# A gated feed-forward layer made as [feature, token] behind a saturated TensorE, with half of its butterflies on GpSimd

## The chip, the cores and the metric

The kernel runs on one core of a Trainium2 chip. The metric is the device time of one execution in microseconds, as the median of several runs. TensorE is written PE, VectorE DVE, ScalarE ACT, GpSimd POOL and SyncE SP; PEld is TensorE's loading of stationary weights.

## The reference

Four batches of 512 tokens with 512 features pass through two layers; each has an attention part and a feed-forward part, gated by a tanh and added to `x`. The change lies in the feed-forward of the first layer, and in the weights of the second one's. The first feed-forward is

```python
def fwht(x):            # normalized Walsh-Hadamard transform along the last axis (length a power of 2)
    ...
def act_quant(x):       # per token
    scale = 127.0 / clip(max(abs(x), axis=-1, keepdims=True), 1e-5)
    return clip(round(x * scale), -128.0, 127.0) / scale
def weight_quant(w):    # ternary
    scale = clip(mean(abs(w)), 1e-5)
    return clip(round(w / scale), -1.0, 1.0) * scale
def h_bitlinear(x, w):
    return einsum('bsh,oh->bso', act_quant(fwht(x)), weight_quant(w))
gate = h_bitlinear(h, w_gate)          # 512 -> 2048
up = h_bitlinear(h, w_up)              # 512 -> 2048
out = h_bitlinear(silu(gate) * up, w_down)   # transform over 2048, then 2048 -> 512
x = x + tanh(g_ffn[0]) * out
```

with `h` the layer norm of `x`. The second feed-forward has the same ternary weights and 8-bit activations, no Hadamard transform, and one weight matrix `w_gv` for both halves.

## The kernel before

Tokens are worked on in tiles of 128; a batch has four. Three strands of work exist.

- `attention` is the second layer's attention: 4 batches of 8 pairs of heads with 4 steps each, 128 steps. It is written as a generator and sets the beat of the program. Its PE work is f32 (`pqh` L769, `pb` L784, `pr` L755, `pss` L828, `ppt` L850, `pc` L858, `po` L870). In a pair, DVE finds the row maxima `nm` (L836), ACT exponentiates (L839) and scales (L842), DVE multiplies `ro` and `rs` by the tables (L792, L794, L797) and POOL adds them (L798); PE's `pr` needs these sums.
- The background. For batches 1 to 3 `before(b)` makes first `adjacency(b)` (the first layer's attention, mostly `max` and `match_replace` on DVE at L454 and L459) and then `feed0(b)`, the first feed-forward. Then `last_weights` quantizes the second feed-forward's weights (called w1) and makes `feed1` of batches 0 to 2. Each of these generators yields estimated costs, and a loop over the attention's steps (L994) takes so many of their pieces as are due. `hidden_T(b)`, which starts a batch's attention, needs the batch's `feed0`.
- The start and the end. Batch 0's adjacency and `feed0`, and the quantization of the first feed-forward's weights, stand ahead of the attention; `feed1` of batch 3 stands behind it. There the flag `alone[0]` is true, more PSUM banks and buffers are lent to the feed-forwards, and `quick` is true in `feed0`.

The program order gives priorities; a scheduler with a cost model then puts the instructions of each engine in an order at build time. On the chip every engine takes its own instructions in that order, and an instruction that waits holds up what stands behind it.

`feed0(b)` first makes, for each tile, `zq`: the normalized, transformed, quantized and transposed activations as [feature, token] in bf16, and the columns `dg` and `du` (one scale for each token). Then `tiles` weaves `gated` of tile j with `back` of tile j - 1 (`woven`, one piece of each in turn).

`gated` makes the inner layer as [token, feature]: in each of four blocks of 512 features, `pg` and `pu` are four accumulated products each, with `zq` stationary and the ternary fp8 weights `wa` moving, 512 columns wide. ACT makes `sg` = silu(dg * pg) out of PSUM, the scale being one number a partition (L312); DVE multiplies by `pu` into `ya` (L313).

`back` then transforms over 2048 features. Its upper four levels are butterflies between chunks of 128 features, an addition and a subtraction of 128x1024 each, on DVE (L556). Its lower seven levels are a product with a 128x128 Hadamard matrix, for which `ya` must be [feature, token]: PE transposes 16 chunks into `ph` (L562), ACT copies them to `yT` (L564), PE multiplies into `pzh` (L568), ACT scales into `yb` (L569). `projected` quantizes, turns by DMA (L202) and multiplies by `wd` (L404).

The background has two PSUM banks while `alone[0]` is false (`bg_ps`, tag `bg`): `pg`, `pu`, `ph`, `pzh` and `pd` of the feed-forwards and the adjacency's products share them. `front_t` gives three and `gate_t` two buffers of 128x512.

`ternary` quantizes weights: a sum of absolute values by ACT (L239), then for each 128x2048 piece a scaling with a rounding constant (L252) and a sign (L253) on ACT. `hold` is true for the first feed-forward's weights, whose pieces stay in SBUF, and false for w1, whose twelve pieces are loaded twice.

Of the kernel before, what the change touches and what calls it, by code (L numbers as in the profile page):

```python
# [34 lines left out]
def flamingo_kernel(  # L35
# [37 lines left out]
    def bg_ps(name):  # L73
        return psb.tile([P, 512], F32, tag="bg", name=name)
# [22 lines left out]
    def back_t(name):  # L97
        return two_k("back", 2, name)
# [121 lines left out]
    def ternary(specs, names, hold):  # L220


        found = []

        def piece(src, inner, i, name):
            t = big(f"{name}{i}")
            marks["load"] = nc.sync.dma_start(
                t if inner == 1 else t.rearrange("p (c o) -> p c o", c=inner), src(i)
            )
            return t  # L230

        for (src, inner, n, dst, count), name in zip(specs, names):
            acc = small.tile([P, n], F32, tag=f"wacc{n}", name=f"acc_{name}")
            held = []
            for i in range(n):
                t = piece(src, inner, i, f"sa_{name}")
                held.append(t)
                junk = bp.tile([P, FF], BF, tag="q", name=f"ja_{name}{i}") if hold else t
                nc.scalar.activation(junk, t, AF.Abs, accum_out=acc[:, i : i + 1])  # L239
                yield 4.0  # L240
            tot = small.tile([P, 1], F32, tag="wtot", name=f"tot_{name}")
            nc.vector.tensor_reduce(tot, acc, AX.X, ALU.add)
            pt = bg_ps(f"pt_{name}")
# [4 lines left out]
            nc.vector.reciprocal(inv, sc)  # L248
            found.append(sc)
            for i in range(n):  # L250
                t = held[i] if hold else piece(src, inner, i, f"sb_{name}")
                nc.scalar.activation(t, t, AF.Identity, scale=inv, bias=magic[:, 0:1])  # L252
# [47 lines left out]
    def gated(u, zq, wa, dg, y):  # L300

        for o in range(4):
# [10 lines left out]
            nc.vector.tensor_tensor(y[:, o * 512 : (o + 1) * 512], sg, pu, ALU.mult)  # L313
            yield 0.9

    reached = []

    def tiles(name, ready, wa, back, spread):
# [4 lines left out]
        def gate(j):  # L323
            zq, dg, du = ready[j]
            y = big(f"ya_{name}_{j}")
            return gated(f"{name}_{j}", zq, wa, dg, y), back(j, y, du)

        def go(gen, parts):
            for _ in range(parts):
# [175 lines left out]
    def feed0(b, w):  # L505
# [44 lines left out]
        def back(j, ya, du):  # L550
            u = f"f{b}_{j}"
            yb = big(f"yb_{u}")

            for src, dst, g in ((ya, yb, 8), (yb, ya, 4), (ya, yb, 2), (yb, ya, 1)):
                for args in butterfly(src, dst, "p (g t q) -> p g t q", {"g": g}):
                    nc.vector.tensor_tensor(*args)  # L556
                    yield 1.3
            for k in range(4):
                pt = bg_tr(f"ph_{u}_{k}")
                for c in range(4):  # L560
                    at = (4 * k + c) * P
                    nc.tensor.transpose(pt[:, c, :], ya[:, at : at + P], ident)  # L562
                hT_ = back_t(f"yT_{u}_{k}")
                nc.scalar.copy(hT_, pt.rearrange("p c q -> p (c q)"))  # L564
# [579 lines left out]
```

## Time and profile before

| | us |
|---|---|
| median of 3 runs | 2050.27 (2046.98 to 2051.11) |
| the profiled execution | 2050.43 |
| its span in the trace | 2048.7 |
| PE busy | 1834.1 (90%) |
| DVE busy | 1584.0 (77%) |
| ACT busy | 1128.1 (55%) |
| POOL busy | 337.0 (16%) |

Mean granted PE clock: 0.973. Busy times are of one core's engines within the span. An f32 product shows as two records, one for each pass. A matmul's duration contains its way through the array, so the spacing of starts, not the duration, tells how fast PE takes them. In a row of a group, the numbers after the count are the busy time, the mean duration in ns and the idle time before these instructions with what ended it. A wait is put down to what came last.

The stages of the span: batch 0 and the first weights until about 260 us; adjacency of batch 1 to 457, its feed0 to 660; of batch 2 to 874 and 1073; of batch 3 to 1288 and 1488; w1's quantization to 1600; feed1 of batches 0 to 2 beside the attention to about 1960; then the last batch's feed1.

### The profile page before, as it was taken

What the parts mean: (1) busy time and instruction counts of PE and PEld (TensorE: products, weight loads), DVE (VectorE), ACT (ScalarE), POOL (GpSimd) and SP (SyncE); (2) the same over time, 40 slices, a digit from 0 to 9 for tenths busy, and PEclk for the clock granted to TensorE, in tenths of its full rate; (3) what the DMA queues carried; (4) which work ended last, traced back from release to release, by engine and by line L of the source; (5) the groups of instructions that cost most, each with busy time, mean ns of one, the idle gap of its engine ahead of it and who ended that gap; (6) DMA issues with size and microseconds to landing.
All of it is one profiled execution on the core that took longest, in us unless ns stands there. A gap on an engine that the chain in (4) does not pass through costs nothing. (4 is left out here: it accounts for less than half of the span.)

```text
span 2048.7 us, 20950 instructions
## 1 busy us (share of the span) xinstructions
PE 1834.1 (90%) x6890; PEld 854.8 (42%) x6890; DVE 1584.0 (77%) x3233; ACT 1128.1 (55%) x1883; POOL 337.0 (16%) x316
## 2 busy tenths in 40 slices
PE   1268799989999999999999999999989999999898
PEld 0035534434444444444444444445443444444333
DVE  7989599987775999976678999766745756866775
ACT  6935454455644455454454554545699565555544
POOL 3020031123101122130121221301211210101000
PEclk9779899999999999999999999999999999999999
DMA  7451021111112222111122121111666112222111
GB/s 274 150 179 38 1 77 42 56 50 32 44 35 48 86 73 73 38 39 35 43 53 84 57 84 47 34 35 38 212 224 235 55 38 71 68 54 66 21 31 42
DMA packets 115548, 151.77 MB, mean 74 GB/s; under 512 B 57456, under 2 KB 68080, under 8 KB 112368
## 3 DMA queue, kind: packets, MB, share of 16 engines
q1 hardware_dynamic: 109968, 134.51, 22.3%
q0 software_dynamic: 4320, 14.16, 1.9%
q10 hardware_dynamic: 1152, 1.77, 0.2%
q8 instruction: 55, 0.90, 0.2%
q14 instruction: 53, 0.43, 0.1%
HBM read 117.90 MB, written 19.92 MB: 67 GB/s over the span
## 5 line engine op out<-in xcount | busy, mean ns | idle before, releaser
L798 POOL TENSOR_TENSOR ro<-ro,rs 128x512 f32<-128x512 f32 x192 | 256.5, 1339 | 1151.8 <-DVE rs L794 704.3
L839 ACT ACTIVATE pp<-pss,nm 128x512 f32<-128x512 f32 x256 | 174.5, 685 | 242.9 <-DVE nm L836 242.2
L769 PE MATMUL pqh<-hT,wq 128*128 128x512 f32 x512 | 238.6, 602 | 5.1 <-ACT pp L839 5.0
L858 PE MATMUL pc<-pT,kv 128*128 128x512 f32 x512 | 231.8, 597 | 1.2 <-ACT pT L851 1.2
L870 PE MATMUL po<-om,cxo 128*128 128x512 f32 x512 | 230.7, 596 | 0.0
L836 DVE TENSOR_REDUCE nm<-pss 128x1 f32<-128x512 f32 x256 | 167.5, 681 | 50.5 <-PE pss L831 50.1
L784 PE MATMUL pb<-qh,wc 128*128 128x512 f32 x384 | 190.9, 614 | 13.1 <-ACT qh L774 8.2
L454 DVE MAX8 m<-work 128x8 f32<-128x512 f32 x304 | 198.2, 681 | 0.6
L459 DVE MATCH_REPLACE8 work<-m,work 128x512 f32<-128x512 f32 x288 | 193.0, 675 | 0.1
L842 ACT ACTIVATE pp<-pp,rsm 128x512 f32<-128x512 f32 x256 | 178.1, 722 | 22.1 <-DVE rsm L841 22.0
L851 ACT COPY pT<-ppt 128x512 f32<-128x512 f32 x256 | 142.3, 590 | 37.3 <-PE ppt L850 37.3
L850 PEld LDWEIGHTS ppt<-ident,pp 128*128 128x128 f32 x1024 | 118.8, 142 | 92.4 <-issue 37.3
L850 PE MATMUL ppt<-ident,pp 128*128 128x128 f32 x1024 | 148.1, 279 | 6.0 <-ACT pp L842 2.8
L875 DVE SCALAR_TENSOR_TENSOR x<-po,gt,x 128x512 f32<-128x512 f32 x128 | 94.4, 743 | 75.5 <-PE po L870 74.8
L828 PE MATMUL pss<-kr,qr 64*128 64x512 f32 x256 | 144.3, 645 | 4.6 <-ACT pp L839 3.9
L831 PE MATMUL pss<-kr,qr 64*128 64x512 f32 x256 | 144.4, 645 | 1.0 <-DVE ro L792 0.5
L769 PEld LDWEIGHTS pqh<-hT,wq 128*128 128x128 f32 x512 | 93.0, 191 | 124.1 <-issue 86.8
L870 PEld LDWEIGHTS po<-om,cxo 128*128 128x128 f32 x512 | 94.4, 190 | 115.1 <-issue 97.0
L858 PEld LDWEIGHTS pc<-pT,kv 128*128 128x128 f32 x512 | 93.7, 190 | 111.5 <-issue 97.2
L792 DVE TENSOR_TENSOR ro<-pb,cos_q 128x512 f32<-128x512 f32 x192 | 130.5, 680 | 10.8 <-PE pb L784 9.9
L863 ACT COPY cxo<-pc 128x512 f32<-128x512 f32 x64 | 37.6, 588 | 149.6 <-PE pc L858 149.6
L755 PE MATMUL pr<-ro,wr 128*64 128x512 f32 x192 | 99.2, 612 | 15.3 <-POOL ro L798 12.5
(266 smaller groups left out, 3012.6 us busy)
## 6 DMA issues: line engine op xcount, KB each, us to landing
wq<-in_wqh SPq DMA_DIRECT2D x64, 256.0 KB, 2.6
om<-omd SPq DMA_DIRECT2D x64, 256.0 KB, 2.8
wc<-in_wkcq SPq DMA_DIRECT2D x32, 384.0 KB, 3.1
krd<-krs POOLq DMA_DIRECT2D x32, 256.0 KB, 2.4
kr<-krd SPq DMA_DIRECT2D x32, 256.0 KB, 2.7
sa_w1v<-in_gvT SPq DMA_DIRECT2D x8, 1024.0 KB, 5.8
sb_w1v<-in_gvT SPq DMA_DIRECT2D x8, 1024.0 KB, 5.1
wr<-in_wqr SPq DMA_DIRECT2D x32, 192.0 KB, 2.4
```

What stands on the lines that cost most here:

```text
L454: nc.vector.max(m8[j], cur[j])
L459: nc.vector.match_replace(works[j], m8[j], cur[j], GONE)
L769: nc.tensor.matmul(pq, self.wqs[i][:, c, :], hT[self.b][:, c, :], start=(c == 0), stop=(c == NC - 1),)
L784: nc.tensor.matmul(pb, self.wc[:, at : at + P], self.qhs[i if i < 2 else o], start=True, stop=True)
L798: nc.gpsimd.tensor_tensor(ro, ro, rs, ALU.add)
L831: nc.tensor.matmul(*args, start=True, stop=True)
L836: nc.vector.tensor_reduce(nm, pss[i], AX.X, ALU.max, negate=True)
L839: nc.scalar.activation(pp, pss[i], AF.Exp, bias=nm, accum_out=sm)
L842: nc.scalar.activation(pp, pp, AF.Copy, scale=rs)
L850: nc.tensor.transpose(pt[:, l, :], pp[:, l * P : (l + 1) * P], ident)
L858: nc.tensor.matmul(pc, kv[self.b][:, l, :], self.pT[i][:, l, :], start=(l == 0), stop=(l == NT - 1),)
L870: nc.tensor.matmul(po, self.cxo[i][:, j * P : (j + 1) * P], self.oms[i], start=(i == 0), stop=(i == 1),)
```

## The change

Three edits.

1. `gated_turned` takes the place of `gated` in `feed0` of batches 1 to 3. It makes the inner layer as [feature, token]: the weights are stationary, `zq` moves, 128 columns at a time, so a block has 32 products instead of 8. The gate's scale now differs from column to column. A row of it is made once a tile: `dg` spread over 128 columns on DVE, turned by one f32 product with the identity, copied by ACT. DVE multiplies `pg` by this row, ACT applies silu in SBUF, DVE multiplies by `pu`. `back` then needs no transposes and no copies for these batches: `ya` goes to the Hadamard product as it is.
2. The subtraction of each butterfly goes to POOL for all tiles of batches 1 to 3 and for tiles 1 and 2 of batch 0. The additions stay on DVE.
3. The scaling of w1's pieces (L252, where `hold` is false) goes from ACT to DVE.

```diff
@@ ternary
-                nc.scalar.activation(t, t, AF.Identity, scale=inv, bias=magic[:, 0:1])
+                if hold:
+                    nc.scalar.activation(t, t, AF.Identity, scale=inv, bias=magic[:, 0:1])
+                else:
+                    nc.vector.tensor_scalar(t, t, inv, MAGIC, ALU.mult, ALU.add)
@@ new function
+    def gated_turned(u, zq, wa, dg, y):
+        row = front_t(f"dgr_{u}")
+        nc.vector.tensor_scalar(row[:, :P], ones, dg, None, ALU.mult)
+        pt = bg_ps(f"pdg_{u}")
+        nc.tensor.matmul(pt[:, :P], row[:, :P], ident, start=True, stop=True)
+        nc.scalar.copy(row[:, P : 2 * P], pt[:, :P])
+        row = row[:, P : 2 * P].unsqueeze(1).to_broadcast([P, 4, P])
+        for o in range(4):
+            pg = gate_ps(f"pg_{u}_{o}")
+            pu = gate_ps(f"pu_{u}_{o}")
+            for pw, at in ((pg, FF + o * 512), (pu, o * 512)):
+                for f in range(4):
+                    cols = slice(at + f * P, at + (f + 1) * P)
+                    for c in range(NC):
+                        nc.tensor.matmul(
+                            pw[:, f * P : (f + 1) * P], wa[:, c, cols], zq[:, c, :],
+                            start=(c == 0), stop=(c == NC - 1),
+                        )
+            sg = gate_t(f"sg_{u}_{o}")
+            nc.vector.tensor_tensor(
+                sg.rearrange("p (f t) -> p f t", f=4), pg.rearrange("p (f t) -> p f t", f=4), row, ALU.mult
+            )
+            nc.scalar.activation(sg, sg, AF.Silu)
+            nc.vector.tensor_tensor(y[:, o * 512 : (o + 1) * 512], sg, pu, ALU.mult)
+            yield 0.9
@@ tiles
-            return gated(f"{name}_{j}", zq, wa, dg, y), back(j, y, du)
+            made = gated_turned if spread and not alone[0] else gated
+            return made(f"{name}_{j}", zq, wa, dg, y), back(j, y, du)
@@ feed0, back
+            shared = not quick or j in (1, 2)
...
-                for args in butterfly(src, dst, "p (g t q) -> p g t q", {"g": g}):
-                    nc.vector.tensor_tensor(*args)
+                for k, args in enumerate(butterfly(src, dst, "p (g t q) -> p g t q", {"g": g})):
+                    (nc.gpsimd if k and shared else nc.vector).tensor_tensor(*args)
                     yield 1.3
             for k in range(4):
-                pt = bg_tr(f"ph_{u}_{k}")
...
-                hT_ = back_t(f"yT_{u}_{k}")
-                nc.scalar.copy(hT_, pt.rearrange("p c q -> p (c q)"))
+                if quick:
...
+                else:
+                    hT_ = ya[:, 4 * k * P : 4 * (k + 1) * P]
```

More of the change, by code (lines that the diff above doesn't have):

```diff
@@ L552, in back @@
             yb = big(f"yb_{u}")
+            shared = not quick or j in (1, 2)
             for src, dst, g in ((ya, yb, 8), (yb, ya, 4), (ya, yb, 2), (yb, ya, 1)):
-                for args in butterfly(src, dst, "p (g t q) -> p g t q", {"g": g}):
-                    nc.vector.tensor_tensor(*args)
+                for k, args in enumerate(butterfly(src, dst, "p (g t q) -> p g t q", {"g": g})):
+                    (nc.gpsimd if k and shared else nc.vector).tensor_tensor(*args)
                     yield 1.3
             for k in range(4):
-                pt = bg_tr(f"ph_{u}_{k}")
-                for c in range(4):
-                    at = (4 * k + c) * P
-                    nc.tensor.transpose(pt[:, c, :], ya[:, at : at + P], ident)
-                hT_ = back_t(f"yT_{u}_{k}")
-                nc.scalar.copy(hT_, pt.rearrange("p c q -> p (c q)"))
+                if quick:
+                    pt = bg_tr(f"ph_{u}_{k}")
+                    for c in range(4):
+                        at = (4 * k + c) * P
+                        nc.tensor.transpose(pt[:, c, :], ya[:, at : at + P], ident)
+                    hT_ = back_t(f"yT_{u}_{k}")
+                    nc.scalar.copy(hT_, pt.rearrange("p c q -> p (c q)"))
+                else:
+                    hT_ = ya[:, 4 * k * P : 4 * (k + 1) * P]
                 pz = bg_ps(f"pzh_{u}_{k}")
```

## The prediction

> **What bounds the kernel now.** First the page's slices, to see which engine is full where.
>
> ```profile
> PE   1268799989999999999999999999989999999898
> ...
> DVE  7989599987775999976678999766745756866775
> ACT  6935454455644455454454554545699565555544
> POOL 3020031123101122130121221301211210101000
> ```
>
> A digit is 51 us. From slice 6 to 36 TensorE (PE) is full whatever the other engines do. VectorE (DVE) fills three times (an adjacency each, batches 1 to 3) and is at 6 to 7 between them, where feed0 runs; ScalarE (ACT) reaches 9 once, around 1500 us. Next, the busy time by stage: the columns are PE, weight load, DVE, ACT, POOL, then granted clock.
>
> ```profile
> 457.00:660.00 203.00, 194.83 (x811) 95.88 (x811) 140.42 (x234) 98.73 (x178) 33.61 (x32) 0.97 0.16 40
> ...
> 874.00:1073.00 199.00, 193.53 (x821) 96.64 (x822) 141.97 (x237) 98.61 (x182) 37.84 (x32) 1.00 0.17 44
> ...
> 1288.00:1488.00 200.00, 192.84 (x819) 96.31 (x819) 142.43 (x239) 111.81 (x196) 36.92 (x31) 1.00 0.30 86
> 1488.00:1600.00 112.00, 104.46 (x331) 46.30 (x330) 60.73 (x134) 109.65 (x146) 21.62 (x17) 0.97 0.62 211
> ```
>
> The first three are feed0 of batches 1 to 3: PE 96%, DVE 70%, POOL 18%. The last is w1's quantization, ACT 98% busy. Busy PE is not PE at full pace, so I priced each PE record of a stage at the closest spacing the timeline shows for its kind (0.429 us for a 512-column f32 pass, 0.215 for 512 fp8 columns, 0.109 for a 128-column f32 pass) and divided by the stage: 0.87, 0.91 and 0.89 in the feed0 stages, 0.83 in w1's, 0.915 from 1600 to 1900. So PE's own work sets about nine tenths of the time, and in w1's stage ACT takes a further share. The chain of waits reaches back only to 1695 us and says nothing of the stages changed. Last, the groups that the change touches (count, then busy and mean ns):
>
> ```profile
> L556 DVE TENSOR_TENSOR yb_f<-ya_f 128x1024 f32<-128x1024 f32 x64 | 77.0, 1233 | 3.7 <-PE ph_f L562 3.6
> ...
> L313 DVE TENSOR_TENSOR ya_f<-sg_f,pu_f 128x512 f32<-128x512 f32 x64 | 43.6, 682 | 25.5 <-PE pu_f L307 21.3 <-ACT sg_f L312 4.2
> ...
> L562 PE MATMUL ph_f<-ident,ya_f 128*128 128x128 f32 x256 | 40.7, 289 | 0.4 <-DVE ya_f L556 0.3
> ...
> L564 ACT COPY yT_f<-ph_f 128x512 f32<-128x512 f32 x64 | 37.0, 584 | 26.1 <-PE ph_f L562 26.1
> ...
> L252 ACT ACTIVATE sb_w1v<-sb_w1v,magic,wi_w1v 128x2048 f32<-128x2048 f32 x8 | 16.7, 2098 | 0.3 <-DVE wi_w1v L248 0.3
> ```
>
> **Part 1, the layer turned (12 tiles).** Removed: 12 x 16 transposes on PE at 0.109 = 20.9 us, and 48 ACT copies x 0.584 = 28 us. ACT is half busy here, so the copies count nothing. Split: each of 48 blocks had 8 products of 512 columns (8 x 0.215 = 1.72 us) and gets 32 of 128 columns, each with new weights. The nearest row is the bf16 transpose, also 128 columns with a weight load each:
>
> ```profile
> 2006.79 0.83 PE L207 MATMUL ptq_hg<-identb,q_g 128*128 128x128 bf16 x12
> 2007.46 0.38 PE L307 MATMUL pg_g<-wa_w,zq_g 128*128 128x512 fp8e4 x1
> ```
>
> Twelve go in 0.67 us: 0.056 each, though a load alone lasts 0.098. So a block takes 32 x 0.056 = 1.79, and 48 blocks +3.4 us. The Trainium skill ("TensorE: Matmul & The Clock Gate", Back-to-back issue gap) speaks against it: streams of load and product at 128 columns sustain about 81 ns each. By that rule 48 x (2.59 - 1.72) = +42 us, and part 1 is a loss. I take the row, from this chip's own run; the runs in it are 12 long against 32, and the weights bf16, not fp8, so 81 stays the upper end, 0.054 the lower. The scale's row: per tile one f32 product (two passes, 0.22) = 2.7 us on PE, with a DVE op and an ACT copy of 0.2 to 0.6 us each, hidden under pg's products (0.9 us). PE in all: -20.9 + 3.4 + 2.7 = -14.8 us.
>
> New wait: Silu took pg from PSUM with the scale folded in; now DVE multiplies by the row (48 x 0.68 = 33 us), then ACT, then DVE again. Behind Silu on ACT stand Exp and the copies of attention; behind the multiply on DVE stand nm and ro. pu holds one of two background PSUM banks 0.7 us longer, but ph no longer takes one. Net I put this at 0 while DVE has its 30% idle; if DVE fills up, the block's 0.7 us reaches PE, 48 x 0.7 = 33 us at most. Silu from SBUF instead of PSUM (0.722 at L842 against 0.687): 1.7 us on ACT, hidden.
>
> **Part 2, subtractions on GpSimd (56: 48 beside attention, 8 in batch 0).** DVE loses 56 x 1.23 = 69 us. No 1024-wide op on POOL is in the trace: 256 wide takes 0.725, 512 wide 1.264, so a line gives 2.34 us. A level then is add and subtraction side by side, next level after both: 2.4 against 2.44 before, no change, if both can run together. They can't quite:
>
> ```profile
> 1030.23 2.35 DVE L556 TENSOR_TENSOR ya_f<-yb_f 128x1024 f32<-128x1024 f32 x2
> 1032.50 0.68 DVE L836 TENSOR_REDUCE nm<-pss 128x1 f32<-128x512 f32 x1
> 1033.10 2.82 DVE L556 TENSOR_TENSOR yb_f<-ya_f 128x1024 f32<-128x1024 f32 x2
> ```
>
> ```profile
> 1030.46 3.25 POOL L798 TENSOR_TENSOR ro<-ro,rs 128x512 f32<-128x512 f32 x1 [0.21 <-DVE rs L794]
> ```
>
> These are DVE's timeline and a line of POOL's. A POOL add of 1.26 us that starts under two butterflies takes 3.25, ending about 1.2 us after they do, and the next pair takes 2.82 instead of 2.35: 0.47 lost. The reduction, which reads PSUM, is not slowed. The skill's "SBUF — State Buffer" (Who interferes with whom) says why: DVE with two SBUF inputs and a GpSimd op that reads SBUF exclude each other for the whole instruction. The row has a loss of 0.47 us on DVE, because the POOL op was half done; by the rule a level is 1.23 + 2.34 = 3.6 us, and DVE stands 0 (add first) to 2.34 us (subtraction first). As DVE and POOL wait for the same event at each level, either can be first. Bounds for 48 levels: a gain of the 59 us DVE saves (worth little where PE is full) to a loss of 48 x 2.34 = 112 us of DVE. I take the loss seen, 0.47, and let half reach PE: 48 x 0.47 / 2 = 11 us. By the rule at its worst it would be 56, and the sum 2082. Half, because PE is 12.0 of 12 us busy in the existing butterfly stretches (955 to 967), where DVE is as crowded. Queued behind a late add on DVE: nm, rsm and ro; behind a subtraction on POOL: the ro add, on whose last piece PE's pr waits (12 + 7 us in 350 to 1450 now). POOL's share in feed0 goes from 18% to about 18 + 4 x 4 x 2.34 / 200 = 37%.
>
> Batch 0, tiles 1 and 2: DVE is 92 to 100% busy from 150 to 220 us, so up to 8 x 1.23 = 10 us could come off; but there nearly everything on DVE has two SBUF inputs, so exclusion may give it all back. I take -2, ends -8 and +9. The key DMAs issued from POOL (162 to 170 us) go out up to 2.4 us later, with 100 us in hand.
>
> **Part 3, w1's scaling from ACT to DVE.** ACT loses 8 x 2.10 + 4 x 2.16 = 25 us; DVE gains 12 x 1.28 (L387, the same form) = 15 us, at 54% busy. PE is at 0.83 of its pace in these 112 us, against 0.89 in the stage before: 112 x 0.06 = 7 us to regain. The DMA of the pieces lands in 5.1 us and is ahead. Value -7, ends -13 and 0. SP's queue is untouched.
>
> **Sum.** -14.8 + 11 - 2 - 7 = -13 us against the profiled execution's 2050.43 (span 2048.7), which is the median of the runs, 2050.27, within 0.01%. Predicted 2037.
>
> **Rivals.**
> (a) *The shared port decides.* Were the subtraction first at most levels, DVE would be held 2.34 us at 48 levels: 112 - 59 saved + 33 for the multiplies = 86 us more on DVE in 602 us of feed0, from 70% to 85%, in lumps. Place: DVE's queue in the butterflies of batches 1 to 3, then nm, Exp, PE. At 611 to 616 the trace shows what a lump costs: nm late by 5 us, PE idle 2.5 us, its clock halved after. If 0.75 us a level reaches PE, 36 us is lost against 24 gained: 2062. It decides from 24 / 48 = 0.5 us a level. For: the rows above. Against: most of attention's DVE work reads PSUM, and runs beside POOL.
> (b) *Weight loads decide.* At 81 ns: 2037 + 38 = 2075. For: load 0.098 alone. Against: 0.056 in every run of transposes.
> (c) *Nothing but moved waits.* PE's saving becomes waits on the longer pg, DVE, ACT, DVE chain; only part 3 is left, and is offset by the port: 2049.
> (d) *The port costs nothing,* and the relieved DVE and ACT close half of the pace lost in feed0 (602 x 0.11 = 66 us is not to be had, 8 is): 2050 - 15 - 2 - 7 - 8 = 2018.
>
> **How the numbers follow.** Forecast 0.40 (2024 to 2046), (d) 0.14, (c) 0.14, (a) 0.22, (b) 0.10. About 0.2% (4 us) is what a measurement of this kernel tells from no change. Faster: forecast, (d), a little of (c): 0.56. Same: most of (c): 0.12. Slower: (a) and (b): 0.32. Cases of both signs hold much, so the range goes from below (d), 2010, to past (a), 2068, leaving out (b) and the far tails. The likeliest case alone: 2024 to 2046.
>
> **What would show it.** No ph_f transposes but 64, and no yT_f copies but 16. Turned products spaced 0.056 (b: 0.08). POOL subtractions of 2.3 us alone and 3.5 where blocked; adds of 1.2, or of up to 3.6 if (a). ACT near 75% in w1's stage, and that stage 7 us shorter. Distance from batch 1's psim to batch 2's (667 to 1080 us) shorter by 3 to 5 us; equal or longer speaks for (a) or (b). I am wrong if PE's pace in feed0 falls below 0.87.

## The result: 46 us slower, and the profile after

The changed kernel takes 2096.04 us (median of 5 runs, 2093.85 to 2099.19) against 2050.27 (2046.84 to 2052.03): a ratio of 1.0228 (95% interval 1.0212 to 1.0245). The prediction was 2037, with a range up to 2068. The profiled execution took 2093.85, its span is 2092.1.

The stages say where it is lost. From the first `pn_f` product of a feed0 to the first `phT` product of `hidden_T`, feed0 of batches 1, 2 and 3 took 201.7, 197.9 and 199.6 us before, and 202.2, 218.0 and 218.7 after. Adjacency, start and end differ by at most 3 us. So nearly all of it lies in feed0 of batches 2 and 3, and batch 1, which makes the same instructions, lost nothing: an explanation has to account for that too.

The page's slices of the changed kernel:

```profile
PE   1278799998999999988899999988889999999888
...
DVE  7989699987776999877659999777567556866685
ACT  6935543454434544544344554533686565555544
POOL 3014031133441211332411221425111110111000
```

TensorE now has slices of 8 where feed0 runs, VectorE is no fuller than it was, and GpSimd shows the subtractions as pairs of 3 to 4. By stage (columns as before: length, PE, weight load, DVE, ACT, POOL, then granted clock; the stages are those of this kernel):

```profile
457.00:660.00 203.00, 184.04 (x1135) 104.39 (x1136) 149.08 (x236) 87.57 (x162) 77.00 (x48) 1.00 0.16 41
875.00:1093.00 218.00, 193.16 (x1146) 109.68 (x1146) 153.24 (x240) 90.61 (x168) 75.12 (x48) 0.97 0.16 40
1309.00:1528.00 219.00, 191.67 (x1145) 109.39 (x1146) 154.90 (x245) 106.46 (x186) 75.24 (x48) 0.97 0.29 91
1528.00:1644.00 116.00, 106.79 (x342) 47.10 (x342) 83.52 (x172) 86.68 (x134) 23.79 (x18) 0.96 0.53 181
```

In batches 2 and 3 PE is 88% busy, against 96% before; DVE is at 70%, as it was; POOL has doubled to 34%. No engine became full. PE waits, and the groups say for what:

```profile
L590 DVE TENSOR_TENSOR ya_f<-yb_f 128x1024 f32<-128x1024 f32 x36 | 81.9, 2278 | 4.1 <-POOL yb_f L590 3.8
...
L590 DVE TENSOR_TENSOR yb_f<-ya_f 128x1024 f32<-128x1024 f32 x36 | 66.0, 1835 | 17.6 <-PE pzh_f L606 12.1 <-POOL ya_f L590 4.2 <-PE ph_f L598 1.3
...
L606 PE MATMUL pzh_f<-had_sb,ya_f 128*128 128x128 f32 x384 | 51.8, 292 | 11.3 <-DVE ya_f L590 10.4 <-ACT yb_f L607 0.9
L335 PE MATMUL pu_f<-zq_f,wa_w 128*128 128x128 bf16 x768 | 50.7, 219 | 21.7 <-DVE ya_f L344 21.5
L335 PE MATMUL pg_f<-zq_f,wa_w 128*128 128x128 bf16 x768 | 50.7, 219 | 10.1 <-DVE sg_f L340 10.1
```

Three waits of PE for DVE are new: 21.5 + 10.1 + 10.4 = 42 us, about as much as the loss. And DVE's additions, 1233 ns before, last 1835 and 2278 ns on average: the 72 butterfly operations left on DVE take 147.9 us, where 128 of 1.23 took 157. DVE got rid of 56 subtractions and of 9 us.

What that looks like, beside tile 0's butterflies in batch 2, in DVE's timeline (start, duration):

```profile
920.16 1.22 DVE L590 TENSOR_TENSOR yb_f<-ya_f 128x1024 f32<-128x1024 f32 x1
921.30 0.68 DVE L340 TENSOR_TENSOR sg_f<-pg_f,dgr_f 128x512 f32<-128x512 f32 x1
921.90 3.35 DVE L590 TENSOR_TENSOR ya_f<-yb_f 128x1024 f32<-128x1024 f32 x1
925.17 0.67 DVE L344 TENSOR_TENSOR ya_f<-sg_f,pu_f 128x512 f32<-128x512 f32 x1
925.76 3.05 DVE L590 TENSOR_TENSOR yb_f<-ya_f 128x1024 f32<-128x1024 f32 x1
928.74 0.68 DVE L340 TENSOR_TENSOR sg_f<-pg_f,dgr_f 128x512 f32<-128x512 f32 x1
929.34 3.05 DVE L590 TENSOR_TENSOR ya_f<-yb_f 128x1024 f32<-128x1024 f32 x1
```

beside it POOL's:

```profile
921.81 2.35 POOL L590 TENSOR_TENSOR ya_f<-yb_f 128x1024 f32<-128x1024 f32 x1 [2.87 <-DVE yb_f L590]
925.39 2.35 POOL L590 TENSOR_TENSOR yb_f<-ya_f 128x1024 f32<-128x1024 f32 x1 [1.23 <-DVE ya_f L590]
```

and PE's:

```profile
922.53 1.06 PE L335 MATMUL pg_f<-zq_f,wa_w 128*128 128x128 bf16 x16
925.89 1.05 PE L335 MATMUL pu_f<-zq_f,wa_w 128*128 128x128 bf16 x16 [2.31 <-DVE ya_f L344]
...
929.47 1.05 PE L335 MATMUL pg_f<-zq_f,wa_w 128*128 128x128 bf16 x16 [1.61 <-DVE sg_f L340]
```

The subtraction starts 0.09 to 0.37 us ahead of the addition of its level, and the addition ends only when the subtraction has ended: they run one after the other, 1.2 + 2.35. The next tile's multiplies (L340, L344) stand in DVE's queue behind each level; PE's next block needs the PSUM bank that such a multiply frees, and waits 1.6 to 2.3 us. Where DVE comes first, as in tile 3, POOL is the one held (3.40 us), and DVE waits for it at the next level:

```profile
1017.85 1.22 DVE L590 TENSOR_TENSOR yb_f<-ya_f 128x1024 f32<-128x1024 f32 x1 [3.56 <-PE pzh_f L606]
...
1021.32 1.23 DVE L590 TENSOR_TENSOR ya_f<-yb_f 128x1024 f32<-128x1024 f32 x1
...
1024.78 1.23 DVE L590 TENSOR_TENSOR yb_f<-ya_f 128x1024 f32<-128x1024 f32 x1 [2.11 <-POOL ya_f L590]
...
1028.24 1.22 DVE L590 TENSOR_TENSOR ya_f<-yb_f 128x1024 f32<-128x1024 f32 x1 [1.91 <-POOL yb_f L590]
1029.38 3.37 DVE L419 TENSOR_SCALAR yb_f<-yb_f,s_hf 128x2048 f32<-128x2048 f32 x1
```

Either way a level takes 3.46 to 3.58 us, against 2.44 for the two operations on DVE alone.

Two of PE's gaps in batch 2 are longer. Beside tile 1's butterflies PE waits 3.6 us for `ya`; behind tile 2's slow scaling (L419), which holds attention's `x` in DVE's queue, it waits 3.2 us. PE's timeline, then the windows behind these gaps (columns as above):

```profile
970.75 3.75 PE L606 MATMUL pzh_f<-had_sb,ya_f 128*128 128x128 f32 x16 [3.61 <-DVE ya_f L590]
...
1034.73 1.22 PE L866 MATMUL pss<-kr,qr 64*128 64x512 f32 x1 [3.16 <-DVE x L913]
```

```profile
969.50:976.50 7.00, 5.75 (x20) 4.51 (x21) 3.34 (x6) 3.88 (x8) 0.02 (x1) 0.53 0.00 0
...
1033.50:1040.50 7.00, 5.77 (x8) 2.50 (x9) 4.83 (x9) 2.66 (x6) 0.00 (x0) 0.54 0.65 150
```

The granted clock is at half for about 7 us behind each. Batch 3 has the same two gaps (3.6 us at 1401, 3.2 us at 1465) with the same dips behind them; in this kernel's gaps of 2.0 to 2.3 us, one in each feed0, the clock stayed at 1.00. With this, batch 1 can be accounted for. From one batch's first `phT` to the next one's (its adjacency and its feed0), before and after; the last column is an estimate, one minus the granted clock, summed over windows of 2 us:

| batch | length, us | PE idle | PE busy | lost to the lower clock, at most |
|---|---|---|---|---|
| 1 | 398.6, 399.1 | 19.7, 30.6 | 378.9, 368.5 | 5, 0 |
| 2 | 413.2, 433.2 | 15.0, 35.3 | 398.2, 397.9 | 0, 7 |
| 3 | 414.8, 434.8 | 17.7, 38.3 | 397.1, 396.5 | 0, 7 |

PE waits more in batch 1 too, 11 us. There the lighter work of the turned layer shows as less busy time, and a stretch at half clock that the kernel before has (behind the gap at 611 to 616 us that the prediction names) is gone. In batches 2 and 3 PE waits 20 us more, and the half clock takes what the lighter work saved.

### The profile page after: what moved, and what is told of

The parts are those of the page before. It is cut to its first block, busy times and chain, and to the rows that moved or that the text cites. A ratio compares the mean times of both kernels' runs of the same rounds, so it can differ in the third digit from the quotient of the medians.

```text
span 2092.1 us, 23016 instructions
## 1 busy us (share of the span) xinstructions
PE 1823.3 (87%) x7874; PEld 888.2 (42%) x7874; DVE 1634.2 (78%) x3249; ACT 1080.3 (52%) x1833; POOL 477.5 (23%) x372
## 5 line engine op out<-in xcount | busy, mean ns | idle before, releaser
L836 POOL TENSOR_TENSOR ro<-ro,rs 128x512 f32<-128x512 f32 x192 | 252.3, 1318 | 900.4 <-DVE rs L832 473.2
L807 PE MATMUL pqh<-hT,wq 128*128 128x512 f32 x512 | 242.8, 613 | 5.9 <-ACT pp L877 5.8
L486 DVE MAX8 m<-work 128x8 f32<-128x512 f32 x304 | 197.9, 679 | 0.6
L335 PEld LDWEIGHTS <-wa_w 128*128 128x128 fp8e4 x1536 | 90.1, 98 | 60.2 <-issue 59.1
```

What stands on the lines that cost most here:

```text
L486: nc.vector.max(m8[j], cur[j])
L807: nc.tensor.matmul(pq, self.wqs[i][:, c, :], hT[self.b][:, c, :], start=(c == 0), stop=(c == NC - 1),)
L836: nc.gpsimd.tensor_tensor(ro, ro, rs, ALU.add)
```

## The experiments

All ran beside the kernel before, which took 2049.6 to 2052.0 there; ratios are to it, and microseconds gained or lost are against the kernel before of the same chip. "feed0" is the sum of its three stages, 599 us before and 639 after.

### The three parts alone

e1: the turned layer alone (of the changed kernel, subtractions back on DVE and w1's scaling back on ACT).

```diff
-                    (nc.gpsimd if k and shared else nc.vector).tensor_tensor(*args)
+                    nc.vector.tensor_tensor(*args)
```

> The turned layer alone; all butterflies on DVE and w1's scaling on ACT, as before. Port theory (the subtractions on GpSimd hold DVE's additions): nothing shares the port, PE has 15 us less to do, so 2033 to 2042 us. Chain theory (DVE's multiply ahead of silu holds the two PSUM banks, wherever the subtractions run): 2070 to 2095 us. If both are needed: about 2045 us.

Measured: 2047.75 us, ratio 0.9987 (0.9978 to 0.9997); feed0 598. A gain of 2.7 us.

e2: the subtractions alone, 48 of batches 1 to 3 and 8 of batch 0 (`made = gated`, transposes kept, scaling on ACT).

> The subtractions on GpSimd alone (48 beside attention, 8 in batch 0); the layer made as [token, feature] and w1 as before. Port theory: the holds of 1.8 us are there in the same number, with one DVE step a block less behind them: 2075 to 2100 us. Chain theory: 2045 to 2055 us. If both are needed: 2055 to 2070 us.

Measured: 2090.7 us, ratio 1.0188 (1.0173 to 1.0204); feed0 639. This is the loss: +40 us. PE's waits of this kernel between 457 and 1490 us (total, times, longest):

```profile
PE ph_f L595 <- DVE ya_f L587: 10.5, 4, 3.0
PE pu_f L307 <- DVE ya_f L313: 9.6, 9, 1.8
PE ph_f L595 <- DVE ya_f L313: 7.5, 4, 2.9
```

The start of the span until the first `phT` took 261.9 us against 260.9, so batch 0's eight subtractions gained nothing.

e3: w1's scaling on DVE alone.

> w1's scaling on DVE alone. By the prediction 2043 us. By the trace of the changed kernel, where the stretch from batch 3's end to the end of the program is no shorter than before (561 to 564 us), 2048 to 2053 us.

Measured: 2051.37 us, ratio 0.9997 (0.9987 to 1.0008). Nothing. The stage of w1 (length, PE, weight load, DVE, ACT, POOL), first before, then in e3:

```profile
1490.00:1600.00 110.00, 103.40 (x325) 45.49 (x324) 59.79 (x131) 107.65 (x143) 21.62 (x17) 0.98 0.61 207
```

```profile
1490.00:1600.00 110.00, 103.06 (x317) 44.46 (x316) 79.71 (x160) 82.33 (x128) 23.56 (x17) 0.95 0.59 203
```

ACT fell from 98% to 75%, as forecast, and PE did not become fuller: 103.4 and 103.1 of 110 us.

e4: the changed kernel without subtractions on GpSimd (parts 1 and 3).

> The whole change without the subtractions on GpSimd. Port theory: 2028 to 2042 us, faster than both kernels. Chain theory: 2070 to 2095 us.

Measured: 2049.77 us, ratio 0.9997 (0.9990 to 1.0004). So the subtractions put on top of e4 cost 2096.04 - 2049.77 = 46 us, 6 more than alone. In the traces these 6 are not in feed0, which grows by 39 us in both cases (600 to 639 from e4, 599 to 639 in e2), though the waits for the multiplies L340 and L344 are there with the turned layer only. The changed kernel takes 2 us more than e4 to the first `phT` (260.8 against 259.0) and 5 more from batch 3's opening to the end (564 against 559); why is open.

### Why the turned layer gains only 3 us

e7: e1 without the row and its multiply.

```diff
-            nc.vector.tensor_tensor(
-                sg.rearrange("p (f t) -> p f t", f=4), pg.rearrange("p (f t) -> p f t", f=4), row, ALU.mult
-            )
-            nc.scalar.activation(sg, sg, AF.Silu)
+            nc.scalar.activation(sg, pg, AF.Silu, scale=dg)
```

> The turned layer alone without the row of scales: silu comes straight from PSUM with a scale a partition (wrong values), so the extra DVE step, and the row's product and copy, are left out. If the DVE step ate the 15 us that PE is spared: 2032 to 2038 us. If PE's work in feed0 does not set the time: 2044 to 2050 us, like the turned layer alone (2047.75).

Measured: 2025.88 us, ratio 0.9885 (0.9869 to 0.9901): 23.7 us gained. PE's saving is real, and larger than the 17.5 us that its own terms give without the row (20.9 - 3.4). The row and its step eat 21 of it.

e8: the kernel before without the 192 transposes and 48 copies (`if quick:` ahead of them, `ya` used as it is).

> The kernel before without the 192 transposes and 48 copies of batches 1 to 3; the Hadamard product takes the data unturned (wrong values). PE loses 20.9 us of work and ACT 28 us, nothing is added. If PE's work sets the time in feed0: 2028 to 2034 us. If it does not: 2044 to 2050 us.

Measured: 2018.19 us, ratio 0.9841 (0.9825 to 0.9857): 31.4 us for work priced at 20.9 us. The price was low: from batch 0's opening to batch 3's, PE's busy time falls by 34 us, of which 5 are the stretch at half clock that is gone, and its idle time rises by 4. That leaves about 29 us for 192 transposes, an estimate of 0.15 us each where 0.109 was taken.

e9: e1 with the multiply by the row done into a buffer that nobody reads, silu straight from PSUM.

```diff
+            nc.scalar.activation(sg, pg, AF.Silu, scale=dg)
+            off = front_t(f"off_{u}_{o}")
             nc.vector.tensor_tensor(
-                sg.rearrange("p (f t) -> p f t", f=4), ...
+                off.rearrange("p (f t) -> p f t", f=4), ...
```

> The turned layer alone, with the row made and DVE's multiply done as before but into a buffer that nobody reads; silu comes straight from PSUM (wrong values). DVE has the same 33 us of work, the block's chain is as short as in the kernel before. If the 22 us between the turned layer alone (2047.75) and the one without the row (2025.88) come from the step in the chain: 2026 to 2034 us. If they come from DVE's load: 2042 to 2050 us.

Measured: 2043.31 us, ratio 0.9957 (0.9941 to 0.9973): a gain of 8.7. Between e7 (23.7) and e9 lies the row's own making (2.7 us of PE by the prediction's price, and small operations of DVE and ACT) and DVE's multiply, whose result no one waits for: 15 us in all, with 48 x 0.685 = 33 us of multiplies. How these 15 divide was not tested. Between e9 and e1 (2.7) lies the longer chain PE, DVE, ACT, DVE of a block: 6 us.

e12: e1 with one 128x2048 pass of a tile (`unmagic` in `projected`) moved from DVE to ACT, 15 us off DVE.

> The turned layer alone, with one 128x2048 pass a tile (the removal of the rounding constant ahead of the turn, 1.22 us on DVE) given to ACT for batches 1 to 3, which the turned layer relieves of 28 us of copies. If DVE's load is what eats PE's saving: 2035 to 2043 us, faster than both kernels. If only the step in the chain does: 2045 to 2052 us.

Measured: 2048.82 us, ratio 0.9982 (0.9975 to 0.9989). A gain of 3.2, as e1: work taken off DVE, and put on ACT, returned nothing here.

### Why the subtractions cost 40 us: the held addition, GpSimd's load, PE's order or lateness

e5: e2, but the subtraction takes the sum as an operand, so it starts when the addition has ended and holds it no more.

```diff
+                    if k and shared:
+                        nc.gpsimd.tensor_tensor(args[0], summed, *args[2:])
+                    else:
+                        summed = args[0]
+                        nc.vector.tensor_tensor(*args)
```

> The subtractions on GpSimd alone, but each takes the sum just made instead of its first half (so the values are wrong), and so must wait for DVE's addition: the two never run at once. A level becomes longer, 1.22 + 2.35 us and two signals. Hold theory (a DVE addition that waits for the port keeps attention's work behind it): additions of 1.2 us again, 2045 to 2065 us. Latency theory (what costs is the later end of each level): no better than the 2090.7 us of the subtractions alone, or some us worse.

Measured: 2093.29 us, ratio 1.0211 (1.0196 to 1.0226). The additions take 1.25 us on average, so they are not held, and the loss is 44 us, no less than e2's; a level is as long as in e2, 1.2 + 2.35.

e6: both halves of each butterfly of batches 1 to 3 on GpSimd.

```diff
-                    (nc.gpsimd if k and shared else nc.vector).tensor_tensor(*args)
+                    (nc.vector if quick else nc.gpsimd).tensor_tensor(*args)
```

> Additions and subtractions of batches 1 to 3 both on GpSimd, batch 0 all on DVE, everything else as before. A tile's butterflies then last 8 x 2.35 = 19 us against 10, but no DVE addition stands in DVE's queue; DVE loses 118 us of work. Hold theory: 2045 to 2065 us. Latency theory: 2090 to 2130 us, since each tile's result comes another 5 us later than with the subtractions alone.

Measured: 2089.79 us, ratio 1.0191 (1.0176 to 1.0206). DVE has 118 us less to do and the loss stays at 40: holding DVE is not what costs. A level is 4.7 us here, longer than e2's, at the same loss; that DVE's relief pays for the rest is possible, but no run shows it.

e11: the kernel before with each subtraction of batches 1 to 3 made twice on DVE (a level of 3.66 us, nothing on GpSimd).

> The kernel before with each subtraction of batches 1 to 3 done twice on DVE: a level lasts 3.66 us, as with GpSimd, but it is on the engine whose time the order was made for, and DVE has 59 us more. Order theory: clearly less than the 40 us of the subtractions on GpSimd, in spite of the load: 2055 to 2075 us. Latency theory: 2090 us or more.

Measured: 2078.7 us, ratio 1.0130 (1.0113 to 1.0148): 27 us. A level as long as e2's costs two thirds of e2's loss with GpSimd out of it. But DVE also has 48 x 1.22 = 59 us more to do here, and e11 cannot tell the length of the level from that load: 27 / 59 = 0.46 us a microsecond is close to what e7 and e9 give for DVE work that nobody waits for (15 / 33 = 0.45, the making of the row included).

e10: e2 with `ph`, `yT`, `pzh` and `yb` of batches 1 to 3 given a priority 150 places lower, so that PE takes more of attention's work first.

```diff
+                with (tc.high_priority(offset=-150) if not quick else nullcontext()):
```

> The subtractions alone on GpSimd, with the transposes and Hadamard products of batches 1 to 3 given a priority 150 places lower, so that PE's order, fixed at build time, has some 13 to 20 products of attention ahead of a tile's first transpose, where the subtractions alone have 2 or 3 and the kernel before 5. Order theory (the order was made for a faster GpSimd, and PE waits at the transposes with ready work behind them): 2045 to 2070 us, and few PE waits on the butterflies. Latency theory (later ends of levels delay attention whatever PE's order): 2090 us or more.

Measured: 2169.66 us, ratio 1.0568 (1.0551 to 1.0586): 77 us worse than e2. This overshot, so e15 did the same with 20 places:

> e2 (subtractions on GpSimd), with ph, yT, pzh and yb of batches 1 to 3 given a priority 20 places lower, so that in PE's order some 3 to 8 more of attention's products stand ahead of a tile's first ph, about 2 to 4 us of work: as much as the butterflies are late. e10 did this with 150 places and lost another 79 us; it overshot. (ii) order: at least half of the 40 us comes back, 2055 to 2072. (i) lateness in the chain: nothing comes back, 2085 to 2100. (iii) load and port: nothing, 2087 to 2094.

Measured: 2104.98 us, ratio 1.0267 (1.0251 to 1.0282), 13 us worse than e2. In both, giving PE other work while the butterflies are late brings nothing back; it makes the tile later still. Every variant gets its own order at build time, and only these two shifts of it were tried, so another order that would help is not excluded.

e13: no work moved or added on DVE, ACT or PE; each tile of batches 1 to 3 only has its butterflies' result later, by two small DMAs behind each other.

```diff
+            if not quick:
+                edge = small.tile([P, 4], F32, tag="edge", name=f"edge_{u}", bufs=1)
+                col = ya.rearrange("p (k x) -> p k x", k=4)[:, :, 0]
+                nc.gpsimd.dma_start(edge, col)
+                nc.gpsimd.dma_start(col, edge)
```

> The kernel before, with all butterflies on DVE, and for batches 1 to 3 two tiny DMAs a tile behind the butterflies: four columns of ya to a side tile and back, which changes no value. The tile's ph comes later by two DMA latencies (some 4 us by the traces' small DMAs), and nothing is added to DVE or ACT. If lateness in a serial chain is the cause (i): about as much as e2 a microsecond of delay, that is +35 to +50 us, 2085 to 2100. If it is PE's order (ii): this order is made with the DMAs' latency reckoned in, so PE gets other work meanwhile, and the loss is small: 2050 to 2065. If it is GpSimd's load and port (iii): nothing, 2048 to 2054.

Measured: 2105.13 us, ratio 1.0266 (1.0247 to 1.0285): +54 us. The page's DMA rows (count, KB each, us to landing):

```profile
edge_f<-ya_f POOLq DMA_DIRECT2D x12, 2.0 KB, 2.3
ya_f<-edge_f POOLq DMA_DIRECT2D x12, 2.0 KB, 2.1
```

4.4 us a tile, 12 tiles: 53 us. In the sum the delay comes out one for one, and roughly so by batch: from opening to opening (first `phT` to first `phT`) batches 1, 2 and 3 are 19, 13 and 17 us longer, for 4 x 4.4 = 18 each. GpSimd waits here for the butterflies with attention's `ro` additions behind it in its queue, but PE's waits for those are no longer than before (3.7 us between 457 and 1520, against 4.9 between 457 and 1490), and its waits for the delayed `ya` itself are short:

```profile
PE ph_f L600 <- DMA ya_f<-edge_f: 4.6, 4, 1.8
PE pr L795 <- POOL ro L838: 3.7, 4, 1.1
```

So PE need not be seen waiting for a late tile for the lateness to cost its full length. From batch 0's opening to batch 3's, PE is idle 39 us more and busy 10 us longer. Its longest gaps lie in the last quarters of the three feed0: 10.6 us waiting for `zT`, and 6.3 and 8.0 us waiting for attention's `pp`; by the estimate used above, stretches at half clock take up to 19 us more than before, which is enough for the longer busy time.

e14: the work on GpSimd without the lateness. GpSimd makes the last quarter of each subtraction, DVE the rest.

```diff
+                        cut = 3 * (FF // 2 // g) // 4
+                        nc.vector.tensor_tensor(d[:, :, :cut], x0[:, :, :cut], x1[:, :, :cut], op)
+                        nc.gpsimd.tensor_tensor(d[:, :, cut:], x0[:, :, cut:], x1[:, :, cut:], op)
```

> The kernel before, with only the last quarter of each subtraction of batches 1 to 3 (256 of 1024 columns, about 0.73 us) on GpSimd; DVE makes the addition (1.23) and three quarters of the subtraction (0.95). A level then ends no later than before (2.2 to 2.4 us against 2.44). (i) lateness: no loss, 2040 to 2052. (ii) order: little or no loss, 2048 to 2055. (iii) load and port: GpSimd has 0.73/2.35 = 0.31 of e2's time at work, and so 0.31 of 40 us: about 2062.

Measured: 2051.79 us, ratio 1.0002 (0.9994 to 1.0011): nothing. 45 us of GpSimd operations in the same places cost nothing (DVE is relieved of some 13 us by the same edit, which could hide a small price). Quite without lateness it is not: the butterflies of a first tile take 12.3 us from start to end, against 11.2 before and 14.1 in e2, and at e13's price that microsecond could have cost 13. The last tile's result, by which the next section goes, is not late (188 us).

e16: the same with the turned layer.

> The turned layer (e1, 2047.75) with a quarter of each subtraction on GpSimd as in e14. DVE is relieved of 48 x 0.28 = 13 us, and the level ends a little earlier. (i) 2040 to 2048, the best realizable version if the chain is what counts; (ii) as e1, 2046 to 2050; (iii) e1 and 12 us: 2060.

Measured: 2054.82 us, ratio 1.0018 (1.0007 to 1.0030). Slower than e1 by 6 us; its feed0 stages sum to 605 us. e14's form does not add up with the turned layer, and why is not settled.

### Where the lateness is charged

In a feed0 the tiles form a chain (three `big` buffers, one `zT`, one `q`), and the last tile's result in `x` must be there before `hidden_T` can open the next batch's attention. Batch 2 in the traces: the starts of the last addition into `x` and of the first `phT`, in us from the first `pn_f` product; then the length from the last opening to this one, against before:

| kernel | last tile's `x` | first `phT` | opening to opening | total against before |
|---|---|---|---|---|
| e8, no transposes | 177 | 189 | -9 | -31 |
| before | 188 | 198 | 0 | 0 |
| e14, a quarter on GpSimd | 188 | 200 | +2 | 0 |
| e11, subtractions twice on DVE | 199 | 210 | +12 | +27 |
| e6, both halves on GpSimd | 200 | 210 | +12 | +40 |
| e5, subtraction behind the addition | 202 | 213 | +15 | +44 |
| e2, subtractions on GpSimd | 203 | 213 | +15 | +40 |
| after | 206 | 218 | +20 | +46 |
| e15, `ph` 20 places later | 211 | 220 | +20 | +54 |
| e13, late only | 224 | 232 | +13 | +54 |
| e10, `ph` 150 places later | 249 | 257 | +38 | +118 |

The batch opens 8 to 12 us behind that result in all of them. e13's 224 and 232 contain attention's work left over from a stage before that was 21 us shorter (194 us against 215); its length from opening to opening is the one to compare. These are the two rows for the kernel before (DVE's and PE's timeline):

```profile
1062.96 0.75 DVE L574 SCALAR_TENSOR_TENSOR x<-pd_f,col_f,x 128x512 f32<-128x512 f32 x1 [8.06 <-PE pd_f L404]
```

```profile
1072.67 0.66 PE L726 MATMUL phT<-ident,nq 128*128 128x128 f32 x4
```

and for the changed kernel, whose feed0 began 0.4 us later:

```profile
1081.56 0.75 DVE L612 SCALAR_TENSOR_TENSOR x<-pd_f,col_f,x 128x512 f32<-128x512 f32 x1 [9.25 <-PE pd_f L436]
```

```profile
1093.08 0.66 PE L764 MATMUL phT<-ident,nq 128*128 128x128 f32 x4
```

In batch 1 of the changed kernel the last result comes at 192 us, before at 194: its chain is not late, and the batch does not open late. In batch 2 the chain is lost at the end. Tile 3's butterflies, four levels of 3.46 us, stand between the steps of tile 2's quantization in DVE's queue; tile 2's scaling (L419 above) takes 3.37 us beside the last subtraction, where it took 1.28 before; tile 2's result comes at 171 us instead of 163. The scaling in the kernel before:

```profile
1026.05 1.28 DVE L387 TENSOR_SCALAR yb_f<-yb_f,s_hf 128x2048 f32<-128x2048 f32 x1
```

e17 went the other way: it shortens the chain without taking work from any engine. In the turned layer the first two levels are made block by block, right behind the multiply, and two levels remain for the whole tile.

```diff
+            half = back_t(f"half_{u}_{o}")
+            for src, dst, g in ((sg, half, 2), (half, y[:, o * 512 : (o + 1) * 512], 1)):
+                for args in butterfly(src, dst, "p (g t q) -> p g t q", {"g": g}):
+                    nc.vector.tensor_tensor(*args)
...
+            for src, dst, g in levels if quick else levels[2:]:
```

> The turned layer (e1, 2047.75), all butterflies on DVE. The first two levels are made a block of 512 features at a time, right behind the block's multiply, and only the last two levels stay behind the whole tile. DVE has no less to do (32 short operations of 128x256 for 4 of 128x1024 twice over: about 5.4 us a tile by size against 4.9), but from a tile's last multiply to its pzh only two levels remain instead of four: some 4.9 - 1.4 = 3.5 us less. Lateness theory, at the price of one microsecond a tile and microsecond of lateness: 12 x 3.5 = 42 us at most, and as PE has its own work at nine tenths of its pace, not more than e8's 31: 2015 to 2035. If the chain of tiles does not set the stage: as e1 or a little slower for the longer DVE work, 2046 to 2054.

Measured: 2063.82 us, ratio 1.0067 (1.0044 to 1.0090): 15 us slower than e1, a miss. Its groups on DVE:

```profile
L345 DVE TENSOR_TENSOR ya_f<-half_f 128x256 f32<-128x256 f32 x96 | 38.5, 445 | 0.3
L345 DVE TENSOR_TENSOR half_f<-sg_f 128x256 f32<-128x256 f32 x96 | 37.6, 434 | 0.7
```

A 128x256 operation takes 0.44 us and not the 0.34 reckoned, so DVE has 76.1 - 58.6 = 17.5 us more to do. But the chain did become shorter, and that did not help:

```profile
1050.70 0.75 DVE L614 SCALAR_TENSOR_TENSOR x<-pd_f,col_f,x 128x512 f32<-128x512 f32 x1 [0.48 <-PE pd_f L437]
```

```profile
1076.61 0.66 PE L766 MATMUL phT<-ident,nq 128*128 128x128 f32 x4 [0.77 <-DVE nq L184]
```

The last result is there 178 us into feed0 (which began at 872.2), 10 us earlier than before, and the batch opens at 204, 26 us behind it. So the end of the chain was not the limit in e17; that attention and PE's work were is likely, but no run shows it. Against e1, PE is idle 6 us more between batch 0's opening and batch 3's, and busy 10 us longer, most of it at half clock. If both strands end nearly together in the kernel before, the price is one-sided: a longer chain delays the batch at once, a shorter one leaves the other strand.

e18: the changed kernel with the subtractions of tiles 2 and 3 back on DVE; tiles 0 and 1 keep theirs.

```diff
-            shared = not quick or j in (1, 2)
+            shared = j in (1, 2) if quick else j < 2
```

> The changed kernel, with the subtractions of tiles 2 and 3 of batches 1 to 3 back on DVE; those of tiles 0 and 1 (and of batch 0) stay on GpSimd: half of the work moved, 24 of 48. If only the last tile's end counts, and tiles 0 and 1 have the slack that the trace shows, the last result comes at 188 to 194 us of feed0 again and nearly all of the 46 us comes back: 2046 to 2058. If every tile's lateness is charged, or GpSimd's load and port cost by themselves, about half comes back: 2068 to 2078.

Measured: 2068.77 us, ratio 1.0084 (1.0066 to 1.0101): 17 us lost instead of 46. The last two tiles' subtractions thus cost 27 to 29 us, but the first two tiles' are not free, as the end of the chain alone would have it. In the traces of batch 2, in steps of 40 us (columns as above), first e4, then the changed kernel:

```profile
914.00:954.00 40.00, 37.89 (x264) 22.65 (x262) 27.77 (x41) 14.56 (x27) 0.00 (x0) 1.00 0.18 44
954.00:994.00 40.00, 36.45 (x244) 21.29 (x242) 31.79 (x47) 19.23 (x35) 9.67 (x6) 1.00 0.21 42
994.00:1034.00 40.00, 39.29 (x213) 21.45 (x211) 36.85 (x52) 16.75 (x32) 3.44 (x2) 1.00 0.16 40
```

```profile
914.00:954.00 40.00, 33.70 (x245) 20.71 (x243) 27.64 (x32) 12.27 (x22) 11.76 (x5) 1.00 0.15 39
954.00:994.00 40.00, 34.82 (x228) 21.44 (x227) 32.23 (x46) 17.69 (x33) 13.41 (x8) 0.91 0.14 34
994.00:1034.00 40.00, 31.88 (x228) 19.69 (x226) 31.77 (x30) 12.59 (x20) 24.22 (x9) 1.00 0.05 16
```

PE is idle 4 us more beside tile 0's butterflies (914 to 954), and 7 us more beside those of tile 3 (994 to 1034); between them lies the first stretch at half clock (0.91 from 954 to 994). In the first place it waits for the multiplies behind the levels, though the results of tiles 0 and 1 come about as early as before (78 and 119 us against 78 and 122). What is lost there is attention's time, and e18 says that it is not regained.

So the verdict on the 40 us: a level that takes 3.5 us instead of 2.44, whichever engine is held, is what costs. e2 and e5 show it without regard to who is held, e13 shows that lateness alone costs as much, and e14 that GpSimd's work in these places, without late levels, costs nothing; e11 agrees, but could be DVE's load. It is charged in two ways: PE's waits for the DVE work queued behind a level, and the late end of the chain. e18 shows that the end of the chain alone is not the whole. To both the longer gaps add a stretch at half clock. Open stay three things: why e6, with the longest levels, loses no more than e2; what exactly bounds e17; and whether another order on PE would have hidden part of the lateness.

No version that computes the layer in full gains as much as the 0.2% that the prediction calls the least to be told: e1 (0.9987) and e12 (0.9982) are the best.

## Why the prediction was wrong

**Part 2 failed, and carries the miss.** The step is "I take the loss seen, 0.47, and let half reach PE: 11 us"; e2 measured 40. Both factors were too small. The 0.47 came from a POOL operation that was half done when the butterflies began. Here addition and subtraction of a level mostly start together, so the whole of the shorter one is added: 3.46 to 3.58 us a level, 1.0 to 1.1 above the old 2.44. The rule weighed there ("SBUF — State Buffer", Who interferes with whom, in the Trainium skill), by which two such operations exclude each other for the whole instruction, gave 3.6; this case's trace agrees with it, and the row was the wrong one to take. And not half but four fifths of it reached the end: 48 x 1.06 = 51 us of longer levels, 40 us lost. The reason for "half", that PE had been fully busy beside the existing butterflies, said only that the old levels were covered.

The mechanism was not quite that of rival (a) either. It priced DVE's held time (86 us more on DVE, then nm, Exp, PE). DVE's share did not rise, DVE may be held or not (e5), or be relieved altogether (e6), at the same loss. What was overlooked is a length: how long a tile takes from its last multiply to `ph`, and what stands in order behind it. The prediction asked what a late addition does to attention's `nm` and `ro`; the late ones were the next tile's multiplies, and the end of the chain. It also saw, at 611 to 616 us, that PE's clock was halved behind a gap of 2.5 us, and gave that no price in the sum: in the changed kernel it takes up to 7 us in each of batches 2 and 3.

**Part 1: PE's side held, DVE's did not.** Sixteen turned products last 1.05 us, their own 0.22 included, so 0.055 us apart; 0.056 had been taken, and the 81 ns of "TensorE: Matmul & The Clock Gate" (Back-to-back issue gap) do not appear; rival (b) is out. e7 confirms the saving. But "Net I put this at 0 while DVE has its 30% idle" was wrong by up to 21 us, in which the row's own PE work (priced at 2.7) is contained: 15 with the row and the multiply made but unused (e9), and 6 more for the chain. This is rival (c): in e1 PE is busy 16 us less from batch 0's opening to batch 3's and idle 15 us more, and e4 measured 2049.77 where (c) said 2049. The stated upper end, 33, was nearer than the value. DVE's idle share, with PE waiting for single results out of its queue, was not cover.

**Part 3: -7 became 0.** ACT fell to 75% as stated, the stage became no shorter (146.1 us in e3 from batch 3's opening to feed1's first product on PE, against 144.8). PE's low pace there was put down to ACT because ACT was full, and no wait of PE on ACT had been shown. Half of the 0.06 of pace to be regained is the clock, granted at 0.97 in this stage and at 1.00 in the one before, in the prediction's own lines.

**Batch 0's** -2 was 0, within its ends.

The sum by measured terms: -2.7 (e1) + 40 (e2) + 1 (e3) = +38, and 8 us more in the three together, most of which the traces put outside feed0. Of the signs named in advance, the subtractions' 2.35 us alone and 3.4 blocked, the additions of up to 3.35, and a distance between the two `psim` that grew from 413 to 433 us all spoke for (a). The pace of PE, which was to stay above 0.87, fell to 0.80 in batch 2 by the prediction's prices (175 us of work in 218).

## What to carry to other kernels

Half of a step moved to a slower engine makes the step as long as the slower half, and as long as both together where the two exclude each other: price the length of the step first, and then look at what stands in order behind it on both engines, not at the share of busy time that is freed. Where a background chain ends just as the main strand needs it, lateness is charged nearly in full (e13), and a chain made shorter need not give anything back (e17); the distance between the chain's last result and its first use tells whether the chain's end is what the next section waits for (8 to 12 us in the kernels of the table, 26 in e17). Look at the granted clock behind each new gap of PE as well. A quarter of the operation on the slower engine, sized so that it ends first, was free on the kernel before and brought nothing; on the turned layer it cost 6 us.

## What the runs showed of the hardware

- A 128x1024 f32 operation on POOL takes 2.35 us alone and 3.40 where DVE's addition of 1.22 started 0.04 us ahead of it; where POOL was first, by 0.37 or 0.09 us, DVE's addition took 3.05 or 3.35. A one-input operation of DVE from SBUF to SBUF (L419) was held as well, 3.37 us for 1.28. Multiplies that read PSUM took 0.67 to 0.69 us in the same stretch.
- DVE on 128x256 f32 with two SBUF inputs takes 0.44 us against 1.22 for 128x1024: a quarter of the columns at 36% of the time.
- Extra DVE work beside a PE that is busy 96% of the time, with DVE at 70%, was not free: 15 us for 33 (e9 against e7, the making of the row included), 27 for 59 (e11, where the levels are longer too).
- Behind PE gaps of 3.2 to 3.6 us in feed0 of batches 2 and 3 of the changed kernel the granted clock was at half for about 7 us (0.53 and 0.54 in batch 2); behind that kernel's gaps of 2.0 to 2.3 us in feed0 it stayed at 1.00. In the kernel before it was at half for about 10 us behind a gap of 2.5 us (at 612.8), and in e2 it fell behind a gap of 2.3 us (at 556.6) and not behind one of 2.6 us (at 1368.1), so no length of gap can be given from which it falls.
